# A post-norm decoder layer on one core: a third buffer for a weight product's operand, and four pieces of side work moved

## The chip, the cores and the metric

The kernel runs on one core of a Trainium2 chip. The metric is device time in microseconds of one execution, as the median of several runs. TensorE (PE) multiplies, VectorE (DVE), ScalarE (ACT) and GpSimd (POOL) work on what it leaves, and SyncE (SP) issues DMA transfers. All arithmetic is in float32.

## The reference

One decoder layer for 8 batches of 256 tokens of width 1024, three blocks with a layer norm after each residual addition:

```python
x = layernorm(x + attention(x, w_qkv, w_o))        # causal, 32 heads of 32, 8 key/value heads, rotary
x = layernorm(x + cross(x, ctx, Wq, bq, Wk, bk))   # one head of 1024; values are ctx itself
x = layernorm(x + ffn(x, qweight, lut4, lut8, bias))

def cross(text, features, Wq, bq, Wk, bk):
    Q = text @ Wq.T + bq;  K = features @ Wk.T + bk
    return softmax(Q @ K.T / sqrt(1024)) @ features

def ffn(x, ...):
    w_l = dequant(qweight, lut4, 4)     # a table of 16 values per output, 4 bit planes packed in int32
    w_h = dequant(qweight, lut8, 8)
    return where(norm(x) > 64, x @ w_h.T, x @ w_l.T) + bias
```

The rows' norms never pass 64 with a layer norm of width 1024 ahead, but the kernel must decide that from its data: it computes with `w_l` and has a branch at the end for the other table.

## The kernel before, in words

Nearly every instruction goes through a helper, `InOrder` (line 55), that keeps an engine's instructions in the order in which the program text issues them. So almost all rows of the profile carry its line, L61, and are told apart by the tiles they name. Only transfers that the text issues as `nc.sync.dma_start` may be placed by the scheduler within SP's queue; those issued as `sync.dma_start` stay in order too. The text is written as Python generators, each of which yields after a few instructions; loops take a step of one generator and then some of another, and so decide what stands beside what on each engine. A `1024x1024` product is done by Winograd's recursion once (`winograd`, line 204): seven products of quarters (in the order 1 2 6 5 7 3 4), each in two steps, with operand sums made ahead on DVE or POOL (`make`, `right_side`, `token_sides`). PE writes each into banks named `x` and `z` (`u` and `v` for the keys and values).

**Stage 1 (0 to 312 us): queries, keys and values.** `front(b)` (line 626) yields 32 steps for the first batch, with plain products, and 28 for each other, 228 in all. PE alternates between a group of `x` or `z` for the queries and one of `u` or `v`. ACT copies the first of each accumulator out of PSUM (`acc`, `acc_k`, `v`), DVE adds the others, then `rotate` (line 580) turns the heads by their angles on DVE and POOL, and a closure in the list `later` transposes them and stores `q_d` and `k_d`. PE begins the next batch in the bank `x` as soon as ACT has copied the old one.

Beside this runs `dequant_low` (line 359) for 5 of the 8 column blocks of the feed-forward weight. It takes 128 columns in a cycle of five steps, 200 steps in all:
1. `first`: two DVE instructions, in every second cycle (256 columns at once)
2. `m`: one DVE instruction that masks three bit planes
3. four ACT activations that fill half of `t`; then the predicated copy of 512 columns of the part before
4. four ACT activations for the rest of `t`
5. the predicated copies of 256 and 128 columns of the part before, its transpose `turned`, and in every second cycle four stores to `wf_d`

`t` has two buffers, so a part's activations wait for the transpose of the part two before. The loop over `front` (lines 690 to 709) sets the pace:

```python
            while low_done * (steps - 20) < 195 * (step - 20):
                low_steps(1)
```

At step 160 the loop takes the first step of `weight_product` (line 467) and of `bias_dots` (line 503). The weight product is that of the cross attention's `Wq` and `Wk`: 24 pieces of eight matmuls for a third of 1024 columns; piece `k` needs the tile `wk` of its rows (512 KB). `load` fetches it two pieces ahead into two buffers, and the result goes through ACT (`m`) to `m_d`. After the last batch the rest of `later` is flushed with half pieces of the weight product between (line 711).

**Stage 2 (312 to 839 us): self attention.** After `fetch_qkv(0)` and two pieces of the weight product the loop of line 907 goes over 48 visits, six per batch, each for some heads and 128 queries. A visit's `scores`, `largest`, `exponentials`, `normalise`, `turn` (transposes `tp` of the probabilities `pr`, copied to `pt`) and `values` are spread over four rounds of the loop. `Beside` fills PE's time between with `project(b - 1)` (line 834), the output product of the batch before, and the rest of the weight product. The five remaining steps of `low` are taken in the loop (`low_steps(1)`, line 948), and `run(low)` at `k == 45` ends it. `cross_weights` (line 871) closes the pools of the weight product, loads its result in four quarters and makes the four sums `ms` for Winograd's recursion, at `k` in 45, 47, 48, 49 and 50. The last projection, `project(7)`, runs alone from 814 to 839.

**Stage 3 (839 to 1125 us): cross attention.** For `u` in 0 to 7 the loop from line 1208 goes over the 14 steps `n` of `g_project(u // 2, u % 2)` (line 1010), which multiplies the weight with the context; its first step in every even `u` issues four operand sums of 1024 columns on POOL (`g_sums`). Between stand the keys' biases (`keys`), `norm_h`, `turn` and `values` of an earlier batch, the transposes of `h` (`turn_h`), and the dequantisation of the other three column blocks (`late`, 120 steps), whose tiles lie in free slots of the weights. Its pace is set so that all steps are done by `u == 6`, `n == 10`. After the loop come `turn_h` of batch 6, `turn` and `values` of batch 5.

**Feed-forward (from 1155 us).** `right_side` of the dequantised weight, then `feed_forward` for each batch, with the last two batches' cross attention between the first two.

Of the kernel before, what the change touches and what calls it, by code (L numbers as in the profile page):

```python
# [24 lines left out]
F32 = mybir.dt.float32  # L25
# [7 lines left out]
P = 128  # L33
B, S, D = 8, 256, 1024
NT = B * S // P
KC = D // P
# [11 lines left out]
def run(steps):  # L48
    for _ in steps:
        pass  # L50
# [14 lines left out]
def decoder_layer(  # L65
# [251 lines left out]
    def layernorm(t):  # L317
        mv = small.tile([P, 1, 2], F32, tag="mv", name="mv")
        moments(t, mv[:, 0])
        rs = small.tile([P, 1], F32, tag="rs", name="rs")  # L320
        dve.reciprocal(rs, deviations(mv))
        normed(t, mv[:, 0], rs)
# [140 lines left out]
    m_stack = ExitStack()  # L463
# [3 lines left out]
    def weight_product():  # L467
        def load(n, i):
            if i == 0:
                wq_n = m_pool.tile([P, KC, third], F32, tag="wq", name="wq", bufs=2)  # L470
                sync.dma_start(wq_n, wq[n])
                wqs.append(wq_n)
            wk_i = m_pool.tile([P, KC, P], F32, tag="wk", name="wk", bufs=2)
            sync.dma_start(wk_i, wk[i])
            return wk_i

        wqs = []
        pieces = [(n, i) for n in range(3) for i in range(KC)]
        loaded = [load(*pieces[0]), load(*pieces[1])]
        for k, (n, i) in enumerate(pieces):  # L480
            yield
            wk_i, wq_n = loaded.pop(0), wqs[n]
            ps = bank(m_banks[-1], "xz"[k % 2])[:, :third]
            for q in range(KC):
                matmul(
                    ps,
                    lhsT=wk_i[:, q, :],
                    rhs=wq_n[:, q, :],
                    start=(q == 0),
                    stop=(q == KC - 1),  # L490
                )
                if q == 3:
                    yield
            if k + 2 < len(pieces):
                loaded.append(load(*pieces[k + 2]))
            m = m_pool.tile([P, third], F32, tag="m", name="m", bufs=2)
            act.copy(m, ps)
            nc.sync.dma_start(m_d[i, :, ts(n, third)], m)
            if n == 2:
                u = D - 2 * third  # L500
                nc.sync.dma_start(u_d[ts(i, P)].rearrange("(p o) -> p o", o=1), m[:, u : u + 1])

    def bias_dots():

        bk_bc = m_pool.tile([P, D], F32, name="bk_bc")
        nc.sync.dma_start(bk_bc, bk.partition_broadcast(P))
        rows = [(bq.partition_broadcast(P), bqk)]
        rows += [(wq_t[ts(i, P), :], wqk[:, i : i + 1]) for i in range(KC)]
        for row, to in rows:
            wide = dq.tile([P, D], F32, tag="row", name="wide", bufs=1)  # L510
            nc.sync.dma_start(wide, row)
            yield
            dve.tensor_tensor_reduce(
                wide, wide, bk_bc, 1.0, 0.0, op0=ALU.mult, op1=ALU.add, accum_out=to
            )
# [8 lines left out]
            yield  # L524


    dq = m_stack.enter_context(tc.tile_pool(name="dq", bufs=1))
    bits = const.tile([P, 32], I32, name="bits")

    low = dequant_low(tiles_of(dq, 2), range(EARLY), bits, lut4)  # L530
# [1 line left out]
    def low_steps(n):  # L532
        for _ in range(n):
            next(low, None)
# [158 lines left out]
    for b in range(B):  # L693
        for n, _ in enumerate(front(b), 1):
            step += 1
            while later and later[0][0] <= step:
                later.pop(0)[1]()

            while low_done * (steps - 20) < 195 * (step - 20):
                low_steps(1)  # L700
                low_done += 1
            make(*at.get((b, n), ([], 0)))
            if n == 12 and b + 1 < B:
                begin(b + 1)
            if n in ((16, 19, 22, 25) if b else (20, 22, 24, 26)) and b + 1 < B:
                make(begun[b + 1][1], 1)
            if step == 160:
                next(product)
                next(dots)
# [4 lines left out]
    if len(later) % 2:  # L714
        next(product)
    s1_stack.close()


    w_pool = ctx.enter_context(tc.tile_pool(name="w", bufs=1, side="right"))
# [140 lines left out]
    def cross_weights():  # L860

        m_stack.close()
        pool = ctx.enter_context(tc.tile_pool(name="mq", bufs=1))
        quad = {}
        for kh, dh in ((0, 0), (0, 1), (1, 1), (1, 0)):
            quad[dh, kh] = t = pool.tile([P, 4, 512], F32, name=f"m{dh}{kh}")
            nc.sync.dma_start(
                t, m_d[4 * kh : 4 * kh + 4, :, ts(dh, 512)].rearrange("k p c -> p k c")
            )
        a11, a12, a21, a22 = quad[0, 0], quad[0, 1], quad[1, 0], quad[1, 1]  # L870
        s1, s2, s4 = (pool.tile([P, 4, 512], F32, name=f"ms{i}") for i in range(3))
        mw.extend([None, a11, a12, s4, a22, s1, s2, a21])
        yield
        dve.tensor_tensor(s1, a21, a22, ALU.add)
        yield
        dve.tensor_tensor(s2, s1, a11, ALU.subtract)
        yield
        dve.tensor_tensor(a21, a11, a21, ALU.subtract)
        yield
        dve.tensor_tensor(s4, a12, s2, ALU.subtract)  # L880
        yield

    cross = cross_weights()
# [23 lines left out]
    for k in range(len(visits) + LAG):  # L907
        b = k // EACH
        now, last, older, oldest = (
            visits[k - n] if 0 <= k - n < len(visits) else None for n in range(LAG + 1)  # L910
        )
        if now:
            if k % EACH == 0:
                o_ts[b] = o_pool.tile([P, NST, KC, P], F32, tag="o_t", name="o_t")
            now.scores()
        if k < 8:
            make(w2_sums if k >= 4 else w2_loads, 1)
        if k % 5 == 1 and k <= 41:
            next(dots, None)
        if k == 45:  # L920
            run(low)
        if k in (45, 47, 48, 49, 50):
            next(cross)
        if k >= EACH and k % EACH == LAG and b < B:
            run(beside.steps)
            parts = [(project(b - 1), 15)]
            if b <= 6:
                n = 2 if b <= 5 else 1
                parts.append((products(n), 2 * n))
            beside = Beside(4 * EACH, *parts)  # L930
        for n in range(4):
            if n < 2 and last:
                last.exponentials(1, n)
            if older:
                older.turn(n)
            if n < 2 and now:
                now.largest(n)
            if n >= 2 and now:
                now.exponentials(0, n - 2)
            if n == 0 and oldest:  # L940
                oldest.values()
            if n in (0, 2) and last:
                last.normalise(n // 2)
            beside.fill()
            if n == 1 and k % EACH == 3 and b + 1 < B:
                fetch_qkv(b + 1)
            if n == 2 or n == 3 and k % 4 == 0:
                low_steps(1)
    run(beside.steps)
    a_stack.close()  # L950


    s3_stack = ExitStack()
# [20 lines left out]
    def turn_h(b):  # L974
        h_ts[b] = c1_pool.tile([P, NST, KC, P], F32, tag="h_t", name="h_t")
        return transpose_rows(h_ts[b], h[b])
# [110 lines left out]
        softs[b] = turned  # L1087

    def values(b):
        c_b = c_pool.tile([P, NST, D], F32, tag="c_b", name="c_b")  # L1090
        nc.sync.dma_start(c_b, c[b].rearrange("(c p) d -> p c d", p=P))
        tiles = h.pop(b)
        for st, pt, rsum in softs.pop(b):
            for half in range(2):
                ps = bank(p3, "cross", 3)
                for q in range(NST):
                    matmul(
                        ps,
                        lhsT=pt[:, ts(q, P)],
                        rhs=c_b[:, q, ts(half, 512)],  # L1100
                        start=(q == 0),
                        stop=(q == NST - 1),
                    )
                to = tiles[st][:, ts(half, 512)]
                dve.scalar_tensor_tensor(to, ps, rsum, to, op0=ALU.mult, op1=ALU.add)
            layernorm(tiles[st])
            nc.sync.dma_start(h2_d[NST * b + st], tiles[st])

# [55 lines left out]
        dve.tensor_copy(count, ps[:1, :1])  # L1164

    fetch_h(0)
    run(project(B - 1))
    o_stack.close()
    p3 = s3_stack.enter_context(tc.tile_pool(name="p3", bufs=1, space=PSUM))
    c_pool = s3_stack.enter_context(tc.tile_pool(name="c", bufs=1, side="right"))  # L1170
# [30 lines left out]
    for u in range(B):  # L1201

        i = u - 2
        for n, _ in enumerate(g_project(u // 2, u % 2), 1):
# [14 lines left out]
                begin = turn_h(i)  # L1219
            if i >= 0 and n >= 8:  # L1220
                next(begin, None)
            late_at += 1
            while late_done * (14 * (B - 1) - 4) < late_steps * late_at and late_done < late_steps:
                next(late, None)
                late_done += 1
            if u == B - 1 and n == 10:
# [12 lines left out]
    wf, wf_sums = right_side(dve, b11, b12, b21, b22, t1, t2, b12, t4)  # L1239
    i = B - 3  # L1240
    make(wf_sums, 2)
    run(turn_h(i + 1))
    turn(i)
    values(i)
    fetch_f(0)
    fetch_h(i + 2)
    make(wf_sums)
# [132 lines left out]
```

## Time and profile before

| | |
|---|---|
| median of 3 runs | 1401.69 us (1400.81 to 1402.79) |
| the profiled execution's own time | 1396.73 us |
| its span | 1394.9 us |
| mean granted TensorE clock | 0.99 |
| busy share of PE, DVE, ACT, POOL | 96%, 68%, 47%, 34% |
| bytes moved by DMA | 180.25 MB |

The span is from the first to the last instruction of the profiled execution; its own time holds a little more. Busy times are sums of an engine's instructions. Groups of instructions are named by line, engine, operation and `output<-inputs`; in the timeline a row's start and length are followed by its shape, its number of instructions and, in brackets, the idle time of the engine ahead of it with what ended it. The granted clock is the share of its full clock that TensorE was given in a stretch.

### The profile page before, as it was taken

The numbers are of one execution on the slowest core, as the hardware profiler recorded it, in microseconds if no ns is written. First come the engines' busy times: TensorE is split into PE (matmuls) and PEld (weight loads), VectorE is DVE, ScalarE is ACT, GpSimd is POOL, SyncE is SP. The second block draws the span as 40 slices with busy tenths as digits, with TensorE's granted clock in tenths as the row PEclk, the third lists the DMA queues.
The fourth block names the chain that finished last, engine by engine and source line by source line (L and its number), as shares of the span: only waits on it lengthen the run. The fifth ranks groups of instructions, "written<-read, shape, count | busy, mean of one in ns | idle before, by whom it ended". The sixth has DMA issues, their size and how long they took to land.

```text
span 1394.9 us, 18286 instructions
## 1 busy us (share of the span) xinstructions
PE 1344.5 (96%) x6194; PEld 822.4 (59%) x6194; DVE 949.7 (68%) x1503; ACT 656.1 (47%) x1995; POOL 480.1 (34%) x284
## 2 busy tenths in 40 slices
PE   8999999998999999999998998999999999999996
PEld 4555555555655555555554547887777765544442
DVE  2998889872877777767778746858686565544333
ACT  0455555551866677666777613444444122321120
POOL 2543333310675445354453612202020003243250
PEclk9999999999999999999999999999999999999999
DMA  8345437337741506226135074776687855322201
GB/s 282 69 69 108 80 62 179 53 50 233 283 144 37 187 31 146 79 84 149 44 101 182 1 279 149 140 170 185 195 216 180 206 162 177 106 76 105 76 31 62
DMA packets 189110, 180.25 MB, mean 129 GB/s; under 512 B 134865, under 2 KB 148177, under 8 KB 187089
## 3 DMA queue, kind: packets, MB, share of 16 engines
q1 hardware_dynamic: 189008, 179.00, 45.8%
q8 instruction: 51, 0.84, 0.2%
q14 instruction: 51, 0.41, 0.1%
HBM read 124.41 MB, written 54.55 MB: 128 GB/s over the span
## 4 chain that ended last, share of the span: by engine, by line
PE 85%; DVE 10%; DMA 2%; issue 1%; ACT 1%; SPq 1%; DVEq 0%; ACTq 0%
PE x L61 33%; PE z L61 25%; PE tp L61 11%; PE cross L61 7%; PE sc L61 3%; PE u L61 3%; PE v L61 3%; DVE slot L61 1%; DVE t L61 1%; DVE st L61 1%; DVE h L61 1%; DMA wk<-in_wk 1%; DVE pr L61 1%; ACT t L61 0%; DMA wkv<-in_w_kv 0%
## 5 line engine op out<-in xcount | busy, mean ns | idle before, releaser
L61 POOL TENSOR_TENSOR pr<-pr,rsum 128x1024 f32<-128x1024 f32 x96 | 186.0, 1938 | 245.8 <-DVE rsum L61 199.5
L61 ACT ACTIVATE pr<-pr,nm 128x256 f32<-128x256 f32 (+1 forms) x528 | 235.0, 450 | 60.4 <-DVE nm L61 47.1
L61 ACT ACTIVATE t<-first,lt,diff 128x128 f32<-128x128 f32 x320 | 128.0, 482 | 84.4 <-DVE first L61 51.1
L61 DVE TENSOR_TENSOR pr<-sc,causal 128x1024 f32<-128x1024 f32 x96 | 116.6, 1215 | 70.5 <-PE sc L61 47.5
L61 PEld LDWEIGHTS tp<-ident,pr 128*128 128x128 f32 x800 | 93.5, 141 | 71.6 <-issue 44.9
L61 DVE TENSOR_REDUCE nm<-pr 128x4 f32<-128x1024 f32 (+2 forms) x112 | 123.8, 1106 | 3.8
L61 POOL TENSOR_TENSOR ra<-ra,rb 128x512 f32<-128x512 f32 (+1 forms) x48 | 57.8, 1205 | 195.2 <-DVE rb L61 177.7
L61 PE MATMUL tp<-ident,pr 128*128 128x128 f32 x800 | 118.5, 277 | 6.7 <-DVE pt L61 6.1
L61 ACT COPY pt<-tp 128x512 f32<-128x512 f32 (+1 forms) x144 | 78.1, 558 | 75.4 <-PE tp L61 75.2
L61 PE MATMUL x<-wq,xt 128*128 128x512 f32 x200 | 96.2, 604 | 6.2 <-DMA wq<-in_w_q 6.2
L61 ACT ACTIVATE slot<-slot,lt,diff 128x128 f32<-128x128 f32 x192 | 77.2, 482 | 51.5 <-DVE slot L61 44.7
L61 ACT ACTIVATION_READ_ACCUMULATOR pr<-pr,nm 128x1 f32 x528 | 101.3, 192 | 0.0
L61 ACT ACTIVATE sd<-mv,eps 128x1 f32<-128x1 f32 (+1 forms) x33 | 9.8, 295 | 186.4 <-DVE mv L61 186.4
L61 DVE COPY_PREDICATED t<-m,t 128x512 f32<-128x512 int32 (+2 forms) x120 | 96.0, 800 | 1.9
L61 PE MATMUL x<-w,o_t 128*128 128x512 f32 x192 | 91.6, 602 | 0.8 <-DVE h L61 0.8
L61 PE MATMUL x<-slot,h_t 128*128 128x512 f32 x192 | 86.5, 592 | 0.0
L61 ACT COPY h_t<-tp 128x512 f32<-128x512 f32 x64 | 36.7, 582 | 95.9 <-PE tp L61 95.9
L61 POOL TENSOR_TENSOR slot<-slot,slot 128x1024 f32<-128x1024 f32 x8 | 19.8, 2481 | 173.3 <-DMA row<-in_c 65.8
L61 PE MATMUL x<-wq,wk 128*128 128x342 f32 x192 | 65.3, 489 | 7.4 <-DMA wk<-in_wk 5.4
L61 POOL TENSOR_TENSOR sf<-h_t 128x512 f32<-128x512 f32 x5 | 8.3, 1668 | 179.1 <-ACT h_t L61 179.1
L61 DVE COPY pt<-tp 128x512 f32<-128x512 f32 x64 | 43.2, 675 | 27.1 <-PE tp L61 27.0
L61 PE MATMUL z<-slot,ms 128*128 128x256 f32 x256 | 59.8, 380 | 1.7 <-DVE g L61 1.7
(154 smaller groups left out, 2625.7 us busy)
## 6 DMA issues: line engine op xcount, KB each, us to landing
h_d<-h SPq DMA_DIRECT2D x32, 512.0 KB, 3.6
wk<-in_wk SPq DMA_DIRECT2D x24, 512.0 KB, 5.0
xt<-in_x_t SPq DMA_DIRECT2D x32, 256.0 KB, 4.5
q_d<-turned SPq DMA_DIRECT2D x128, 64.0 KB, 2.2
q_t<-q_d SPq DMA_DIRECT2D x16, 512.0 KB, 6.3
h<-in_x SPq DMA_DIRECT2D x16, 512.0 KB, 6.5
h<-h_d SPq DMA_DIRECT2D x16, 512.0 KB, 4.9
slot<-in_c_t SPq DMA_DIRECT2D x16, 512.0 KB, 7.2
```

The costliest lines, as they stand in the source:

```text
L61: return lambda *args, **kw: self.tc.keep_in_program_order(issue(*args, **kw))
```

## The change

- `wk` has three buffers and is loaded three pieces ahead.
- The tile `wide` of `bias_dots` lies in the pool of the weight product, no longer in that of the dequantisation.
- All 200 steps of `low` are taken in stage 1, its end right after it, and its pool is closed there. Attention takes none.
- The pool of the cross weights' sums `ms` is opened after attention; the quarters are still loaded at `k == 45`, and the four sums are made after attention and at steps 3, 6 and 9 of `project(7)`.
- The late dequantisation begins at `u == 0`, `n == 7` and ends where it did.
- `values` becomes a generator with a step for each half of a tile. Between stage 3 and feed-forward, two of the four steps of `turn_h` (each four transposes into one bank and ACT's copy out of it) stand ahead of `turn`, and the others between the steps of `values`.

```diff
@@ weight_product
-            wk_i = m_pool.tile([P, KC, P], F32, tag="wk", name="wk", bufs=2)
+            wk_i = m_pool.tile([P, KC, P], F32, tag="wk", name="wk", bufs=3)
...
-        loaded = [load(*pieces[0]), load(*pieces[1])]
+        loaded = [load(*pieces[i]) for i in range(3)]
...
-            if k + 2 < len(pieces):
-                loaded.append(load(*pieces[k + 2]))
+            if k + 3 < len(pieces):
+                loaded.append(load(*pieces[k + 3]))
@@ bias_dots
-            wide = dq.tile([P, D], F32, tag="row", name="wide", bufs=1)
+            wide = m_pool.tile([P, D], F32, tag="row", name="wide", bufs=1)
@@
-    dq = m_stack.enter_context(tc.tile_pool(name="dq", bufs=1))
+    dq_stack = ExitStack()
+    dq = dq_stack.enter_context(tc.tile_pool(name="dq", bufs=1))
@@ stage 1
-            while low_done * (steps - 20) < 195 * (step - 20):
+            while low_done * (steps - 20) < 200 * (step - 20):
...
     s1_stack.close()
+    run(low)
+    dq_stack.close()
@@ cross_weights
+        yield
+        pool = ctx.enter_context(tc.tile_pool(name="ms", bufs=1))
         s1, s2, s4 = (pool.tile([P, 4, 512], F32, name=f"ms{i}") for i in range(3))
         mw.extend([None, a11, a12, s4, a22, s1, s2, a21])
-        yield
@@ attention
         if k == 45:
-            run(low)
-        if k in (45, 47, 48, 49, 50):
             next(cross)
...
-            if n == 2 or n == 3 and k % 4 == 0:
-                low_steps(1)
     run(beside.steps)
     a_stack.close()
+    next(cross)
@@ values
     def values(b):
+        run(value_steps(b))
+
+    def value_steps(b):
...
                 dve.scalar_tensor_tensor(to, ps, rsum, to, op0=ALU.mult, op1=ALU.add)
+                yield
@@ stage 3
-    run(project(B - 1))
+    for n, _ in enumerate(project(B - 1), 1):
+        if n in (3, 6, 9):
+            next(cross)
...
-            late_at += 1
-            while late_done * (14 * (B - 1) - 4) < late_steps * late_at and late_done < late_steps:
+
+            late_at += u > 0 or n > 6
+            while late_done * (14 * (B - 1) - 10) < late_steps * late_at and late_done < late_steps:
@@ before the feed-forward
-    run(turn_h(i + 1))
+    begin = turn_h(i + 1)
+    next(begin)
+    next(begin)
     turn(i)
-    values(i)
+    run(in_turn(value_steps(i), begin))
```

## The prediction

> **What bounds the kernel now.** I read the page first, then the chain of waits, then PE's waits by releaser, and last PE's timeline at each of its larger gaps.
>
> ```profile
> span 1394.9 us, 18286 instructions
> PE 1344.5 (96%) x6194; PEld 822.4 (59%) x6194; DVE 949.7 (68%) x1503; ACT 656.1 (47%) x1995; POOL 480.1 (34%) x284
> PE 85%; DVE 10%; DMA 2%; issue 1%; ACT 1%; SPq 1%; DVEq 0%; ACTq 0%
> ```
>
> PE is busy for 96%, so its gaps hold about 50 us. The change leaves PE's instructions and, but for eight transposes, their order as they are. It can win or lose only in PE's gaps and in slow matmuls after them. These are the gaps that it touches (start, duration, and in brackets the idle time before, with its releaser):
>
> ```profile
> 129.53 1.13 PE L61 MATMUL u<-wkv,xt 128*128 128x256 f32 x4 [1.22 <-ACT acc_k L61]
> 275.96 1.13 PE L61 MATMUL u<-wkv,xt 128*128 128x256 f32 x4 [1.30 <-ACT acc_k L61]
> 312.59 6.56 PE L61 MATMUL x<-wq,wk 128*128 128x342 f32 x16 [1.96 <-ACT acc L61]
> 326.59 6.53 PE L61 MATMUL x<-wq,wk 128*128 128x342 f32 x16 [2.83 <-DMA wk<-in_wk]
> 341.42 4.85 PE L61 MATMUL x<-wq,wk 128*128 128x342 f32 x16 [2.58 <-DMA wk<-in_wk]
> 387.28 0.66 PE L61 MATMUL tp<-ident,pr 128*128 128x128 f32 x4 [2.69 <-DVE pt L61]
> 387.77 4.16 PE L61 MATMUL x<-wq,wk 128*128 128x342 f32 x8
> 849.32 5.30 PE L61 MATMUL x<-slot,ms 128*128 128x256 f32 x16 [3.00 <-DVE g L61]
> 891.13 3.72 PE L61 MATMUL x<-t,m 128*128 128x256 f32 x16 [1.98 <-DVE g L61]
> 1133.84 1.14 PE L61 MATMUL tp<-ident,h 128*128 128x128 f32 x8 [1.45 <-ACT h_t L61]
> ```
>
> Sixteen product matmuls take 4.85 us at 341.42 and 6.56 or 6.53 at 312.59 and 326.59: a gap can cost a second time, by 1.7 us. The windows show why (the stretch, its length, then PE busy, PEld, DVE, ACT, POOL, then the granted clock, DMA share, GB/s):
>
> ```profile
> 326.00:330.00 4.00, 3.41 (x7) 2.16 (x8) 0.00 (x0) 0.00 (x0) 0.00 (x0) 0.62 0.93 214
> 341.00:345.00 4.00, 3.58 (x13) 2.43 (x14) 3.97 (x5) 0.00 (x0) 0.00 (x0) 1.00 0.98 361
> ```
>
> **From stage 1 to attention (-5.5).** Both `wk` gaps are waits for a load 2 ahead. SP issues the load at 322.04 behind four `q_d` stores, and the view of DMA issues gives a `wk` load 5.0 us to land. With a third buffer that load is issued a product earlier, at about 317.6 in the new order of SP. The last dequantisation part now needs no new `first`, so PE starts the product at about 310.6 instead of 312.59, and four pieces in a row end at about 329. Then `scores` need `q_t`. In SP's new order `k_t` follows the four `wf_d` stores of the finished dequantisation, two `h` loads and the `wk` load, and is issued at about 326.3; `q_t` behind it takes 6.3 us, so scores start at about 333 instead of 337.66, where the timeline has them: 4.7 won. The next piece has no wait: 2.6 won. The 4 us wait for `q_t` makes one slow stretch: 1.7 lost. Sum -5.6, taken as 5.5; from 2.6 (`q_t` lands late) to 7.2 (no slow stretch).
>
> **Five dequantisation steps leave attention (-4.3).** At 387.28 PE waits for the copy `pt`, which stands in DVE's queue behind three predicated copies of 7.25 us. They go: 2.69, and the slow stretch behind (8 matmuls in 4.16 against half of 4.85) 1.7. Sum 4.4, taken as 4.3 (2.7 to 4.4). The `wide` tile changes its pool only: 0.
>
> **Sums of the cross weights (-0.6).** Four DVE sums of 2.24 to 3.48 us left PE gaps of 0.40 and 0.24 in attention. Beside the last projection DVE has 2.74 us idle in every product of 3.43; a sum of 2.24 and an addition of 0.69 are 2.93 and fit. If POOL's sums stretch it to 3.1 or more it costs up to 1.5.
>
> **Late dequantisation begins later (-4.85 and -0.6).** At 849.32 PE waits for `g`, an addition queued on DVE behind the first dequantisation steps of stage 3 (`first` 2.33 and `m` 2.70 us while POOL makes its sums, against 1.08 and 0.54 without). Begun after that, they cost nothing there: 3.00, and 5.30 against 3.45 for the same sixteen matmuls elsewhere, 1.85. Range 3.0 to 4.9. The pace is 120 steps in 88 places instead of 94, so other steps meet POOL's later sums. The gap of 1.98 at 891.13 stands behind three predicated copies of 7.26 us; in DVE's new order these follow `g`, and the gap goes. One of 1.70 at 955.27 becomes about 1.45 and one of 0.89 at 1040.61 about 1.65, as each takes over the step pattern of the other. That is 4.57 against 3.1, a gain of 1.5; the first is borderline, as the two steps left ahead of `g` may stretch as at 849, so I take 0.6 (a loss of 1.5 to a gain of 2.5).
>
> **Transposes between values (-0.9).** Three gaps before 1150 (1.45, 0.19, 1.28) come from sixteen transposes in a row, faster than ACT evicts them (0.58 each), and from values in a row waiting on DVE. Eight and then four between values leave a good half; some gaps stay as the first eight still stand together. 0 to 1.5.
>
> **Stage 1 takes 200 steps instead of 195 (+10.3).** This is the part that speaks against the change. The steps fall at other places of a batch, and the batch ends have no slack: PE restarts on `x` 0.86 us after the last half `u`, and ACT's copy `acc` ends 0.8 after it. Whatever ACT has queued ahead of that copy PE waits for. These rows of the old ends show it:
>
> ```profile
> 308.88 3.18 ACT L61 ACTIVATE t<-first,lt,diff 128x128 f32<-128x128 f32 x8 [7.55 <-DVE first L61]
> 311.97 0.56 ACT L61 COPY acc<-x 128x512 f32<-128x512 f32 x1
> ```
>
> At 275.96 four activations stand between `acc` and `acc_k`: 1.30; at 129.53 likewise, 1.22. In the new order of ACT, by batch:
> - End of the second: split as in the old rows, but sixteen activations ahead and the fourth group between, 1.2 to 4.0; I take 2.0.
> - End of the third: twenty ahead of `acc`, the last of them waiting for a new `first`. The row above (eight, `first` ready at 308.78) gives a gap of 3.0 beside POOL's sums and a slow stretch of 1.8; the old 1.22 goes. 3.6 (2.7 to 5.2).
> - End of the fifth: four activations ahead of `acc`, waiting for the transpose of the part two before. In the old end of the seventh that transpose ended 2.07 after the last `u` began (273.60 and 0.31, less 271.84) and the activations took 1.55 from 274.01 on, so `acc` would end at 4.3 instead of 0.8: less what PE still has, 2.9, and 1.8 for the clock. 4.7 (1.8 to 5.4).
> - The seventh is split again, 0 (-0.5 to 1). The others show no activations there.
>
> Sum 10.3 (5.2 to 15.6).
>
> **The sum.** Gains 5.5 + 4.3 + 0.6 + 4.85 + 0.6 + 0.9 = 16.75; loss 10.3; net 6.45, say 6.5 faster. The profiled run took 1396.73 (span 1394.9), 5.0 below the median of 1401.69. The sum makes it 1390.2, and the median 1395.2.
>
> A rule is weighed here. The Trainium skill, page "TensorE: Matmul & The Clock Gate", Part 1 on the clock gate, says that the clock is halved after an idle window of about 3.4 us. The rows above disagree: the granted clock was 0.62 after 2.83 us idle, though 1.00 after 2.58. By the page none of these gaps would cost a second time: the gains would be 3.9 + 2.6 + 0.6 + 3.0 + 0.6 + 0.9 = 11.6, the loss 10.3 less two stretches of 1.8, 6.7, and the sum 4.9 faster, 1396.8.
>
> **Rivals.**
> 1. *Stage 1's batch ends cost no more than before* (loss 2.0 instead of 10.3, so 14.75 faster, 1387). DVE is busy 30 to 36 of 37 us per batch there; if it runs even 2 us ahead at the two bad ends, the activations are over before `u`. For it: ACT is idle over half of the stage. Against it: the rows show ACT waiting for DVE's `first` and `turned` at just these ends.
> 2. *The third buffer only moves the wait* (1398). The loads are no longer late, but `q_t` waits behind two `h` loads of 512 KB and the stores, so scores start as late as before; the first part is worth 2.6 instead of 5.5, 3.6 faster in all. For it: 0.93 of the DMA's time is taken at 326.
> 3. *Slower: activations ahead of the accumulator's copy at four batch ends instead of two* (1406). If the ends of the second and the seventh come out like those of the third and fifth, each at 5.3 with its slow stretch, the loss is 21.2 against 16.75. It decides from a little over three such ends. For it: the orders there differ by four activations only, less than DVE drifts in a batch. Against: both were split before, at 1.2 to 1.3.
>
> **How the numbers follow.** A measurement of this kernel tells 0.2% (2.8 us) from no change. My forecast has 0.45, with 1390 to 1399 for itself; rival 1 0.18 (all faster); rival 2 0.12 (half of it within 0.2%); rival 3 0.25 (0.20 slower by more, 0.05 within). Of the forecast's own chance 0.40 is faster by more than 0.2% and 0.05 within. Faster: 0.40 + 0.18 + 0.06 = 0.64; same 0.05 + 0.06 + 0.05 = 0.16; slower 0.20. The range takes in rival 1 with 2 us to spare and the lower half of rival 3: 1385 to 1405.5; 0.05 lies below and 0.13 above.
>
> **What would show it.** Right: no `wk` among PE's waits; scores at about 333 less what stage 1 shifts (they are to be read against the start of the weight product); no gap of 2 us at 387 and 849 on the old clock; gaps of 3 us at the ends of the third and fifth batch (near 129 and 203), released by ACT `acc`, with a granted clock under 0.7 behind. Wrong: PE's gaps in stage 1 the same as before (rival 1), a `q_t` wait as long as both `wk` waits (rival 2), more than three gaps of 3 us before 312 (rival 3).

## The result: 0.2% faster, half of the forecast

The changed kernel takes 1398.26 us in the median of 8 runs (1395.44 to 1399.19), the kernel before 1401.49 in 8 runs beside it (1398.83 to 1402.79). The ratio is 0.9979, with a 95% interval of 0.9969 to 0.9988: 3.2 us faster, where 6.5 were forecast. The profiled execution took 1396.21 (span 1394.4), only 0.5 less in the span than that of before. Three lines of its page:

```profile
span 1394.4 us, 18286 instructions
PE 1343.7 (96%) x6194; PEld 821.7 (59%) x6194; DVE 935.1 (67%) x1503; ACT 656.5 (47%) x1995; POOL 474.0 (34%) x284
PE 85%; DVE 10%; DMA 1%; ACT 1%; issue 1%; SPq 1%; DVEq 0%; ACTq 0%
```

Nothing is to be seen at this scale: PE's gaps have moved, not gone. PE's waits by releaser (engine, line, waited for, then the sum, the count and the longest) tell where to. Four of the rows:

```profile
PE x L61 <- ACT acc L61: 8.0, 2, 4.7
PE sc L61 <- DMA q_t<-q_d: 4.6, 1, 4.6
PE u L61 <- ACT acc_k L61: 3.6, 2, 1.9
PE tp L61 <- DVE pt L61: 3.4, 2, 2.0
```

The 5.4 us for `wk` and most of those for `g` (3.1 of 7.6 are left) have gone from the list; in their place stand ACT's copies of the accumulators in stage 1, and one wait for `q_t`. PE's timeline has them at the batch ends and at the first scores:

```profile
95.83 1.13 PE L61 MATMUL u<-wkv,xt 128*128 128x256 f32 x4 [1.77 <-ACT acc_k L61]
135.25 3.78 PE L61 MATMUL x<-wq,xt 128*128 128x512 f32 x4 [4.74 <-ACT acc L61]
213.90 1.98 PE L61 MATMUL x<-wq,xt 128*128 128x512 f32 x4 [3.25 <-ACT acc L61]
290.24 1.21 PE L61 MATMUL u<-wkv,xt 128*128 128x256 f32 x4 [1.86 <-ACT acc_k L61]
350.49 2.09 PE L61 MATMUL sc<-k_t,q_t 32*128 32x128 f32 x32 [4.58 <-DMA q_t<-q_d]
```

Since PE's order is nearly the same in both kernels, each matmul's start can be subtracted from its twin's. That shift (after less before) is +16.0 us near the end of stage 1, +12.8 after the first scores, +8.4 at 400, +7.9 at the end of attention, +3.1 at 857, +1.8 at 1043 and -0.6 from 1148 on. The differences between these are what each part made, and they are compared with the forecast's terms further down.

### The profile page after: what moved, and what is told of

Read it like the earlier page. It is cut to its first block, busy times and chain, and to the rows that moved or that the text cites. A ratio compares the mean times of both kernels' runs of the same rounds, so it can differ in the third digit from the quotient of the medians.

```text
span 1394.4 us, 18286 instructions
## 1 busy us (share of the span) xinstructions
PE 1343.7 (96%) x6194; PEld 821.7 (59%) x6194; DVE 935.1 (67%) x1503; ACT 656.5 (47%) x1995; POOL 474.0 (34%) x284
## 4 chain that ended last, share of the span: by engine, by line
PE 85%; DVE 10%; DMA 1%; ACT 1%; issue 1%; SPq 1%; DVEq 0%; ACTq 0%
PE x L61 32%; PE z L61 25%; PE tp L61 12%; PE cross L61 7%; PE sc L61 4%; PE u L61 3%; PE v L61 2%; DVE t L61 2%; DVE slot L61 1%; DVE st L61 1%; DVE h L61 1%; ACT t L61 1%; DVE first L61 1%; DVE rb L61 1%; DVE turned L61 0%
## 5 line engine op out<-in xcount | busy, mean ns | idle before, releaser
L61 PE MATMUL x<-wq,xt 128*128 128x512 f32 x200 | 100.0, 625 | 14.2 <-ACT acc L61 8.0
L61 DVE COPY_PREDICATED t<-m,t 128x512 f32<-128x512 int32 (+2 forms) x120 | 87.1, 726 | 2.2 <-ACT t L61 0.3
L61 PEld LDWEIGHTS x<-wq,xt 128*128 128x128 f32 x200 | 39.2, 199 | 43.8 <-issue 31.3
L61 PE MATMUL x<-wq,wk 128*128 128x342 f32 x192 | 62.0, 468 | 0.5 <-ACT m L61 0.5
```

What stands on the lines that cost most here:

```text
L61: return lambda *args, **kw: self.tc.keep_in_program_order(issue(*args, **kw))
```

## Experiments: stage 1 and the place of the activations

**The old pace with the rest of the change** (`pace195`):

```diff
-            while low_done * (steps - 20) < 200 * (step - 20):
+            while low_done * (steps - 20) < 195 * (step - 20):
```

> The changed kernel with the old pace of 195 in stage 1; the last five dequantisation steps then stand right behind stage 1. Theory (at the batch ends of stage 1 activations stand ahead of the accumulator's copies, and this costs 16 us in the trace of the changed kernel): stage 1's gaps are again those of the kernel before (1.2, 1.3 and 2.0 at the ends of the third, seventh and eighth batch), the weight product starts near 312.6 instead of 326.4, and of the 13.8 some 1 to 3 are given back to the five steps behind stage 1: 1386 (1384 to 1389). Rival (the expected gain went elsewhere: the parts behind stage 1 gave less than reckoned): within 3 of the changed kernel's 1398.

Measured: 1391.92, ratio to before 0.9945 (0.9930 to 0.9959). Stage 1's gaps are those of before and the product starts at 312.90, as the theory said; but the time is 6 above its value, and 6 below the rival's. PE's timeline tells why:

```profile
345.38 2.09 PE L61 MATMUL sc<-k_t,q_t 32*128 32x128 f32 x32 [11.30 <-DMA q_t<-q_d]
```

The scores came 32.5 us after the product's start, against 24.1 in the changed kernel. The run `pace195_low_first` below takes this up.

**The pace alone in the kernel before** (`pace200alone`): the opposite edit, 195 to 200, and nothing else.

> The kernel before with one number changed, the pace of stage 1 from 195 to 200. Theory: stage 1 loses what it loses in the changed kernel (13.8 up to the start of the weight product), the slow stretch at 312 (1.7) and the gap and slow stretch at 387 (4.4) go, so it is slower than before by about 7 to 8: 1409 (1406 to 1412). Rival: within 3 of 1401.5.

Measured: 1407.49, ratio 1.0060 (1.0044 to 1.0076), within the theory's range. Its trace repeats the changed kernel's gaps in stage 1 (1.77, 4.73, 3.26 and 1.87). The longest, at the end of the third batch:

```profile
135.05 3.14 PE L61 MATMUL x<-wq,xt 128*128 128x512 f32 x4 [4.73 <-ACT acc L61]
```

So the number 200 by itself makes the loss of stage 1.

**Holding the activations back** (`hold`): the changed kernel, but the third and fourth step of the cycle wait at a batch's end.

```diff
-            while low_done * (steps - 20) < 200 * (step - 20):
+            late_in = 0 < b < B - 1 and n > 23 or b == 0 and n > 27
+            for _ in range(2):
+                if low_done * (steps - 20) >= 200 * (step - 20):
+                    break
+                if late_in and low_done % 5 in (2, 3):
+                    break
                 low_steps(1)
                 low_done += 1
```

> The changed kernel, but the steps that issue activations are held back in the last five steps of a batch of stage 1 and caught up with at the next batch's start, two at a time at most. All 200 steps stay in stage 1. Theory: it is the place in ACT's queue and not the number of steps that costs; no gap over 2 us at a batch end, the product starts at 310 to 313, 1383 (1381 to 1387). Rival (DVE's and ACT's load in stage 1 is simply too high with 200 steps): the gaps go to the starts of the batches, and the time stays within 4 of 1398.

Measured: 1381.57, ratio 0.9870 (0.9853 to 0.9887), about 15 us below the changed kernel. All 200 steps are still in stage 1, and the gaps at the ends of the second to the seventh batch are gone. ACT's timeline at the end of the third batch, first of the changed kernel, then of this one:

```profile
131.54 3.18 ACT L61 ACTIVATE t<-first,lt,diff 128x128 f32<-128x128 f32 x8 [10.34 <-DVE first L61]
134.63 0.56 ACT L61 COPY acc<-x 128x512 f32<-128x512 f32 x1
```

With the hold:

```profile
128.66 0.59 ACT L61 COPY acc<-x 128x512 f32<-128x512 f32 x1 [8.46 <-PE x L61]
129.53 0.37 ACT L61 COPY acc_k<-u 128x256 f32<-128x256 f32 x1 [0.28 <-PE u L61]
130.52 3.19 ACT L61 ACTIVATE t<-first,lt,diff 128x128 f32<-128x128 f32 x8 [0.63 <-DVE first L61]
```

In the first, ACT had been idle for 10.34 us, the copy stood behind eight activations that waited for `first`, and PE waited behind the copy. In the second the same eight follow it. It is the place in the queue that costs, not the load. One gap was made by the hold itself: 5.22 us at 67.3, just behind the end of the first batch.

## Experiments: from stage 1 to attention

**A third piece before the first scores** (`hold_3pieces`): `run(products(3))` instead of 2, and `products(9)` later instead of 10, on top of `hold`.

> As the one that holds the activations back, and three pieces of the weight product instead of two between the start of the loads of q_t and the first scores; attention has one piece fewer to fill with. If the wait for q_t (4.6 us and a slow stretch of 1.7 behind it) is one for a transfer that comes when it comes, a piece of 4.8 us fills it: 5 to 6 below the kernel that only holds, 1378. Rival: attention lacks the piece, or the third piece delays the loads behind it: no gain, within 2 of it.

Measured: 1376.93, ratio 0.9836 (0.9822 to 0.9851). The wait for `q_t` is gone, and a piece fits where it was: the scores come 24.0 us after the product's start with five pieces ahead of them, 23.7 with four in `hold`.

**Two buffers for `wk` again** (`two_buffers`): the part of the change in its name, undone alone.

> The changed kernel with two buffers for wk again, loaded two pieces ahead; all else as changed. If the third buffer is worth what the forecast gave it (5.5 with the earlier start of the product, some 3.5 without): 1401 to 1402, with gaps of 2.5 to 2.9 released by wk in front of the third to fifth piece. Rival (the wait only moves to q_t, which is issued behind the stores whatever wk does): 1398 to 1399, the wait for q_t shorter by what wk's gaps take.

Measured: 1394.74, ratio 0.9964 (0.9950 to 0.9977). This is below both forecasts. Undoing the third buffer does not make the kernel slower; the times make it 2 faster, with intervals that overlap. In the traces the shift against the changed kernel's first goes from -1.4 before the product to -3.4 after the fifth piece. PE's timeline:

```profile
337.05 6.43 PE L61 MATMUL x<-wq,wk 128*128 128x342 f32 x16 [2.54 <-DMA wk<-in_wk]
343.32 4.77 PE L61 MATMUL z<-wq,wk 128*128 128x342 f32 x16
348.02 1.17 PE L61 MATMUL sc<-k_t,q_t 32*128 32x128 f32 x32
349.99 4.84 PE L61 MATMUL x<-wq,wk 128*128 128x342 f32 x16 [0.80 <-DMA wk<-in_wk]
```

The waits for `wk` are back, and the scores wait for nothing. SP's queue shows why, first the changed kernel, then two buffers (the product starts at 326.44 and 325.05):

```profile
339.98 1.95 SPq L383 DMA_DIRECT2D wf_d<-turned  x4
342.04 0.87 SPq L844 DMA_DIRECT2D h<-in_x  x2
343.77 0.33 SPq L61 DMA_DIRECT2D k_t<-k_d  x1
344.14 0.91 SPq L61 DMA_DIRECT2D q_t<-q_d  x2
```

With two buffers:

```profile
337.53 2.11 SPq L383 DMA_DIRECT2D wf_d<-turned  x4
339.75 0.39 SPq L61 DMA_DIRECT2D k_t<-k_d  x1
340.18 1.98 SPq L61 DMA_DIRECT2D q_t<-q_d  x2
```

`k_t` is issued 17.3 us after the product's start with three buffers and 14.7 with two, and two `h` loads stand ahead of it only with three. With three it also waits for a transfer. SP's own waits between 343 and 344.2 us in the changed kernel are one row:

```profile
SPq L61 <- DMA wf_d<-turned: 0.8, 2, 0.5
```

With two buffers SP waits for nothing between 339 and 340.3, around the issue of `k_t`.

**`h` behind `q_t`** (`h_in_order`): the changed kernel with line 844 as `sync.dma_start`, in order.

> The changed kernel with the loads of x into h (line 844) kept in program order, so that they no longer stand ahead of k_t and q_t in SP's queue. Theory 1 (1 MB of h ahead of q_t takes its time on the DMA engines): q_t lands 2.5 to 3 us earlier after the start of the product, the wait of 4.0 to 4.6 falls to 1.5 to 2, 1395 to 1396. Theory 2 (with the third buffer the tiles of k_t lie on memory of the dequantisation, and k_t waits until the last wf_d stores have landed): k_t is issued at the same place, 17.3 after the product's start, and of the wait only what h took of the DMA's time goes. If theory 2 holds alone: 1398.

Measured: 1402.95, ratio 1.0019 (1.0008 to 1.0031), slower than either theory said. At the place in question both hold a part. `k_t` is still issued 17.5 after the product's start with no `h` ahead of it, just after the last `wf_d` stores have landed, and the wait for `q_t` is 2.54, where the changed kernel's two profiles have 4.6 and 4.0. The loss comes later. In attention the `k_t` of a later batch is issued at 549.0, behind two `h` loads, instead of 536.7, and two gaps appear in projections (4.75 us at 564 and 1.45 at 626). How the one leads to the other I did not follow. With `h` in order on the fastest kernel below (`hold_low_first_h`) the same happens, with gaps of 3.39 at 544 and 1.33 at 606:

> The fastest kernel so far (1375.1) with h in order as well. There the third piece covers the wait for q_t already, and what is left at this place are waits for wk of 1.5 and 0.7 us: with 1 MB less on the DMA engines ahead of them they fall to 0 to 1: 1374 (1373 to 1376). Rival: h comes later than project(0) wants it: slower by more than 1.

Measured: 1380.73, ratio 0.9859 (0.9841 to 0.9877); its rival was right, by 5.7 us.

**The dequantisation's end ahead of the stores** (`pace195_low_first`): `pace195` with `run(low)` moved ahead of the loop that flushes `later`.

> The changed kernel with the old pace of 195, and the last steps of the dequantisation taken ahead of the last stores of q_d and k_d instead of after them. With pace 195 alone scores waited 11.3 us for q_t, whose loads came 27.6 after the product's start. If that wait comes from the wf_d stores being issued and landing ahead of k_t, it falls to 4 or less: 1384 to 1386. Rival (the eight activations that now stand ahead of the product's copies, and DVE's copies, delay the stores of q_d as well): 1388 to 1391.

Measured: 1382.33, ratio 0.9876 (0.9858 to 0.9894): 9.6 us from moving one line. `k_t` is issued 18.7 after the product's start instead of 27.6, and the wait ahead of the first scores falls from 11.3 to 2.43 (the profile names no releaser for what is left):

```profile
338.11 1.17 PE L61 MATMUL sc<-k_t,q_t 32*128 32x128 f32 x32 [2.43 <-issue]
```

So what `pace195` lost hung on the place of the dequantisation's end. That its four `wf_d` stores did it, which had to be issued and to land ahead of `k_t`, fits SP's waits for them there (3.4 us in sum), but activations and copies moved with them. The forecast range was too high by 1.7, since the theory allowed for a wait of up to 4.

**All mends together** (`hold_low_first`): `hold_3pieces` without the hold in the first batch, and `run(low)` ahead of the flush.

> As the kernel that holds activations back and has three pieces before the first scores, with two mends from its trace: nothing is held in the first batch (there the hold made a gap of 5.2 us at 68, which costs about 3 more than the 2.2 of before), and the dequantisation ends ahead of the last stores of q_d and k_d, so that its stores to wf_d are not issued after them and ahead of the loads of k_t and q_t. Theory: 3 for the first, 0 to 1.5 for the second, as the third piece already covers most of that wait: 1373 (1371.5 to 1375) against 1377. Rival: without the hold in the first batch the steps shift through all the others, and another end collides: 1375 to 1379.

Measured: 1375.08, ratio 0.9816 (0.9800 to 0.9833), the fastest of all. The 5.22 us gap is gone and stage 1 gains the 3 us, but the trace shows only 0.7 of it left at the end (waits for `wk` of 1.47 and 0.69 us behind the earlier start, and a slow stretch at 1114). The time lies on the border of the theory's range and the rival's.

## Experiments: the smaller parts, and one execution against another

**The late dequantisation begun at once** (`late_at_once`: `late_at += 1` and the denominator with 4, as before).

> The changed kernel with the late dequantisation begun at the first step of stage 3 as before. Theory: the gap of 3.0 us at the second product of stage 3 and its slow stretch of 1.85 come back, and 1.2 in the later ones: 1404 (1402 to 1405). Rival: the gap comes back but without the slow stretch, which depends on more than the gap: 1401 to 1402.

Measured: 1401.73, ratio 1.0015 (1.0003 to 1.0026), 0.36% above the changed kernel's ratio, which is 5.0 us. The bare time lies in the rival's range, but the trace decides: the gap is back, and with it its slow stretch, sixteen matmuls in 5.38 us, where the same row of the changed kernel takes 3.62.

```profile
855.82 5.38 PE L61 MATMUL x<-slot,ms 128*128 128x256 f32 x16 [2.99 <-DVE g L61]
```

**Transposes and values as before** (`values_whole`).

> The changed kernel with the transposes of h, turn and values in a row as before. The traces have 2.4 us of difference between 1040 and 1150 at this place, the forecast 0.9: the one makes 1400.7, the other 1399.2; the trace shows it more closely than the time, as the difference of shifts between 1125 and 1150.

Measured: 1398.52, ratio 0.9989 (0.9977 to 1.0001). The ratios make the part 1.4 and can't tell it from nothing. Between 1125 and 1150 the shift steps by 2.3 against the changed kernel's first profile, but by 0.7 against its second (`after_again`, below). The difference is TensorE's clock behind the same gap of 1.45 us. Windows of three microseconds there (stretch, length, PE, PEld, DVE, ACT, POOL, granted clock, DMA share, GB/s), for the kernel before, then for the changed kernel's first and second profile:

```profile
1136.00:1139.00 3.00, 3.00 (x5) 1.38 (x5) 2.07 (x1) 1.68 (x3) 0.00 (x0) 0.50 0.79 161
1136.50:1139.50 3.00, 3.00 (x11) 1.64 (x11) 2.97 (x2) 0.86 (x3) 0.00 (x0) 1.00 0.91 357
1137.50:1140.50 3.00, 3.00 (x7) 1.38 (x8) 2.97 (x2) 0.37 (x1) 0.00 (x0) 0.66 0.92 336
```

So the new order itself is worth 0.5 to 0.7 us (0.5 by the gaps: 1.45, 0.19 and 1.28 before, 1.45 and 0.95 now). The other 1.7 of the first trace's step are a slow stretch that the changed kernel's first execution did not have and its second had.

**The cross weights' sums in attention** (`cross_early`), in one execution.

> The changed kernel with the sums of the cross weights in attention again (visits 45 to 50). The forecast and the shift between the traces give 0.5 to 0.6 us for this part: gaps of 0.4 and 0.24 come back near 804 and 811, and none in the last projection. In the time it can't be told from the changed kernel.

Measured: 1396.87. Of the two gaps 0.40 at 802 is back. Nothing more can be said.

**Both kernels once more** (`before_again`, `after_again`).

> The kernel before once more, for a second profile. Its first profiled execution was 4.8 us below its median, the changed kernel's 2.0 below its own, and the two spans differ by 0.5 where the medians differ by 3.2. If executions differ by slow stretches of TensorE (granted clock under 0.7) that come after some gaps and not after others, this profile shows the same gaps as the first and other slow stretches, each 1.7 to 2 us. Rival: the gaps themselves differ.

> The changed kernel once more, for a second profile: as for the kernel before, the same gaps within 0.3 us each, with the two gaps over 3 us at the ends of the third and fifth batch, and other slow stretches.

Measured: 1398.98 and 1398.82. The gaps are the same but for those that end with a transfer (4.33 instead of 2.83 for `wk` in the kernel before). What follows a gap is not. The end of the fifth and of the seventh batch in the same kind of windows behind the gap, first in the changed kernel's first profile, then in its second:

```profile
213.90:216.90 3.00, 3.00 (x9) 1.73 (x10) 3.00 (x5) 1.75 (x5) 1.26 (x1) 1.00 0.31 49
290.20:293.20 3.00, 2.96 (x7) 1.79 (x8) 2.97 (x6) 1.53 (x4) 1.68 (x2) 0.66 0.32 48
```

The second profile:

```profile
214.50:217.50 3.00, 2.93 (x4) 1.38 (x5) 2.95 (x5) 1.82 (x6) 1.27 (x1) 0.50 0.33 51
293.60:296.60 3.00, 2.97 (x10) 1.88 (x11) 2.97 (x6) 1.61 (x5) 1.68 (x2) 1.00 0.32 48
```

The same gap of 3.2 us is followed by the full clock in one execution and by half of it in the other (2.7 us more), and the gap of 1.86 us the other way round. So one profiled execution is one draw. The second pair of spans differs by even less than the first, 1397.1 against 1397.0. How much the draw is worth can be read from the executions recorded beside `two_buffers`: of 24 of the kernel before, the fastest took 1395.26 us at a mean granted clock of 0.992, the slowest 1402.29 at 0.987. A clock lower by 0.005 over 1400 us is 7.0 us, the whole difference. The kernel before was profiled at 0.990 and 0.989, above its mean of 0.988 in these 24; the changed kernel at 0.991 and 0.988, around its mean of 0.989 in 8. This is a good part of why the spans differ by 0.5 and 0.1 where the medians differ by 3.2.

## Why the forecast was half right

Each part came out with the sign that was forecast; the sizes of two terms did not. The last two columns are the shifts in the first pair of traces and in the second (`before_again`, `after_again`).

| part | forecast | first pair | second pair |
|---|---|---|---|
| stage 1, 200 steps | +10.3 (5.2 to 15.6) | +16.0 | +16.7 |
| stage 1 to attention, third buffer | -5.5 (-2.6 to -7.2) | -3.1 | -3.5 |
| five steps leave attention | -4.3 | -4.5 | -5.7 |
| cross weights' sums | -0.6 | -0.5 | -0.7 |
| late dequantisation, first sums | -4.85 | -4.85 | -4.9 |
| late dequantisation, later sums | -0.6 | -1.25 | -1.3 |
| transposes between values | -0.9 (0 to -1.5) | -2.4 | -0.7 |
| sum | -6.5 | -0.6 | -0.1 |

**The term that failed is stage 1.** The mechanism was right, and `pace200alone` and `hold` show it; it was mis-sized by 5.7 us, beyond the upper bound. By its steps: the end of the second batch 2.0 against 2.0 measured. The third 3.6 against 6.3: I took the moment at which DVE finishes `first` from the old end of the eighth batch, 0.8 before the last `u`. Here it was 2.0 after. DVE ran later than there, and its second instruction took 1.24 us beside POOL's sum instead of 0.29, as its row shows:

```profile
130.21 1.24 DVE L61 TENSOR_SCALAR first<-first 128x256 f32<-128x256 int32 x1
```

The fifth 4.7 against 3.4 in this execution: its gap was 3.25 where 2.9 was forecast, but the clock was not cut there; in the second one it was, and the same end cost about 6. The seventh 0 against 2.3: split groups there cost a gap of 1.86 instead of 1.30, and a slow stretch that the second execution had not. And 2.0 at places that the forecast had not at all: 1.04 is a gap at 78 for the copy `v`, inside the second batch, and 0.6 arises in the first 12 us, where the change does nothing. I had looked at batch ends only. Rival 3, four bad ends instead of two, did not come: only the third and the fifth have gaps over 3 us, the second and the seventh stayed split, at 1.77 and 1.86.

**The second is the third buffer.** The forecast had the mechanism of rival 2 in its own chain (`q_t` behind `wf_d` and two `h` loads) and still gave the part 5.5. `q_t` was awaited for 4.6 us, and the scores came 24.1 after the product's start against 25.1 before: 2 us are won by the product's own earlier start, and the wait for `wk` is exchanged for one for `q_t`. `k_t` was issued 17.3 after the product's start, where the forecast had 15.7. `two_buffers` shows that the buffer itself is worth nothing here or costs 2. Shown is that `k_t` comes earlier with two, and that SP waits for the `wf_d` stores around its issue with three (0.8 us, and 2.0 in `h_in_order`) and not with two. That this is because the tile of `k_t` lies in the dequantisation's freed memory only with three fits these waits, but was not tried by itself. Rival 2's number, 1398, is the measured one, but by luck: its mechanism was half there, and it had stage 1 as the forecast had it.

**What came out right** are the three gaps released by DVE: 2.69 with its slow stretch at 387, 3.00 with its slow stretch at 849, 1.98 at 891. Each was read as one queue at one place, and each vanished whole. `late_at_once` confirms the second in the time (5.0 measured, 4.85 and 0.6 forecast). The later gaps were to become 1.45 and 1.65 and came at 1.36 and 1.56, so the 0.6 was too careful. For the gap at 849 the forecast set `first` at 2.33 against 1.08, but these are two instructions: the one of 2.33 takes 0.29 elsewhere (at 308.49). The term itself was read from PE's gap, so this did not enter the sum. The transposes were worth about what was forecast; the -2.4 of the first pair holds a slow stretch of 1.7, as `values_whole` showed.

**The sum against the median.** The traces differ by 0.5, the medians by 3.2. The first profile of before was 4.8 us under its median, that of after 2.0 under. The forecast mapped one execution's gain onto the median, and that is good to 2 or 3 us only. In the forecast's own terms the two pairs of traces make 0.6 and 0.1, so half of the forecast in the medians is no sign that its terms were half right.

On the clock, the Trainium skill, page "TensorE: Matmul & The Clock Gate", Part 1, also says that the activity window is free-running, so that where it falls varies from run to run. The runs fit that: one gap, two clocks. They do not fit the page's idle window of about 3.4 us as a threshold: 0.66 was granted behind 1.86 us. The forecast's sum by that page, 4.9 faster, is nearer to the measured 3.2 than its own, but by luck: the slow stretches that it sets at nothing were there, and the wait of 4 us that the forecast had for `q_t` is longer than the page's window.

## What to carry to other kernels

In an engine that works in program order, the place of side work in front of the copy that frees a bank matters more than its amount: keep work that waits for another engine out of the last steps before such a copy (here 15 us of 1400 from holding two kinds of step for five steps of a loop). When a wait for a transfer is removed, look at what stands ahead of the next load in the DMA queue, and at what the new buffer's memory pushes aside. Where only one engine has gaps, fill an unavoidable wait with a piece of its own later work.

## What the runs showed of the hardware

The granted clock after an idle time is not a function of that time alone: behind the same 3.2 us gap it was 1.00 in one execution and 0.50 in another, behind 1.86 us 0.66 and 1.00, behind 1.45 us 1.00 and 0.66, behind 4.74 us 0.50 in both. A slow stretch cost from 1.6 us (6.43 against 4.85 for sixteen matmuls in `two_buffers`) to 3.0 (at 388 in the second profile of the kernel before), and executions of one kernel differ by up to 7 us with it. The kernel without most of these gaps, `hold_low_first`, ran at a mean clock of 0.995 in all five executions, so part of its gain of 26 us is clock that it no longer loses: about 10 us, estimated from 0.995 against 0.988.
